# Two attention layers on one Trainium2 core: regrouping transfers per pair of heads, issued with the copy, and a shorter lag

## The chip, the cores and the metric

The kernel runs on one core of one Trainium2 chip (trn2). All data is float32. The metric is the device time of one execution in microseconds (us). The time before is 4608.19 us, the median of three runs (4605.17 to 4620.24).

## The reference

The input x is (8, 512, 32, 32): 8 images of 512 channels and 1024 positions. Two layers follow each other. Each normalizes its input by groups of 16 channels and adds its output to what came in. Layer 0 is ordinary attention with 8 heads of 64 channels. Layer 1, which the change is about, mixes the heads of the scores before the softmax and normalizes each head's attention matrix after it. Cut to what matters:

```python
def _L1_conv_ref(x, w_q, w_k, w_v, w_head, in_gamma, in_beta, w_proj, b_proj):
    q = jnp.einsum('oc,bct->bot', w_q, xf).reshape(b, heads, hd, t)   # k, v alike
    attn = jnp.einsum('bhdq,bhdT->bhqT', q, k) * scale
    attn = jnp.einsum('gh,bhqT->bgqT', w_head, attn)
    attn = jax.nn.softmax(attn, axis=-1)
    # mean and variance over both axes of each head, then gamma and beta
    attn = (attn - mean) / jnp.sqrt(var + EPS)
    attn = attn * in_gamma[None, :, None, None] + in_beta[None, :, None, None]
    out = jnp.einsum('bhqT,bhdT->bhqd', attn, v).reshape(b, t, c)
    out = out @ w_proj.T + b_proj

x = x + _L0_conv_ref(_gn(x), ...)
x = x + _L1_conv_ref(_gn(x), ...)
```

The mixing of heads, `bhqT->bgqT`, is what shapes the kernel: for each pair of a query and a key the 8 scores of the 8 heads are multiplied by an 8 x 8 matrix.

## The kernel before

The order of the work on each engine is the order in which the program writes it down; no scheduler moves it. Layer 0 runs for all images first, then layer 1 for all images, with the projections of the next image laid between the end of one image and the beginning of the next.

**Layer 1 of one image.** The work is cut into tiles of queries and keys: QB = 256 queries (4 blocks, qb) by KB = 256 keys (4 blocks, kb), so 16 tiles t per image. Each t takes two half steps x = 2t and 2t + 1; there are NX = 32 of them. In a half step PE computes scores of four heads: scores(x, 0) and scores(x, 1) take one pair of heads hp each. One call fills one PSUM tile of 128 x 1024 with 128 partitions of queries, two heads, two groups j of 128 queries, and 256 keys. The queries are laid out so that partition p of the scores is c * 64 + i * 8 + r, with c of 2, i of 8 and r of 8.

**Raw.** The scores leave PSUM for SBUF as they are, into `raw` (line 1204): one tile [128, 8 heads, 2, 256] for a whole t, of which there are two. The copy (lines 1207 and 1209) is on ACT, or on DVE for scores(x, 0) of the first MLAG half steps and of odd ones.

**Regrouping.** To mix heads with a matmul the 8 heads have to lie on partitions. `regroup(t)` (line 1211) does this with 8 SBUF-to-SBUF transfers from the queue of SyncE (SP), one for each r: it reads 16 partitions of `raw` (those with this r, a stride of 8), 16 KB each, and writes 128 partitions (c, i, head) of a tile `re`, 2 KB each. Each r has a tile of its own; there are 16 of them, for two t. All 8 are issued together in the odd half step, after scores(x, 1). The order of r is R_ORDER = (0, 4, 1, 5, ...).

**Mix.** `mix(y, j)` (line 1220) multiplies a piece of `re` by the constant `wmix`, which holds w_head for 8 queries on the diagonal, in 32 small matmuls of 64 x 64 (64 in the profile, since a float32 matmul appears as two) into another PSUM tile. ACT then takes the exponential (line 1237). Mix and exponential belong to half step y = x - MLAG with MLAG = 4, so they run four half steps after the scores of the same data.

**Sums and values.** One half step later still, w = x - MLAG - 1, ACT squares the exponentials (line 1247), DVE adds up the exponentials and their squares (lines 1254 and 1258), and PE multiplies the exponentials by v (`values`, line 1276) into two accumulators. After 8 half steps a block of queries is finished: `totals` sums over the keys with PE, the totals go through a small tile `row` to a column layout by transfers, `reciprocals` and `divide` follow 2 and 5 half steps later, and `leave` takes the accumulators out in the first half step of the next block (four copies on ACT, four on DVE).

**Buffers.** All PSUM tiles of layer 1 but the accumulators come from one pool of three (`m_psum`): scores, mix, totals and projections take turns in the order in which they are written down, so each waits until the reader of the third tile before it is done. The transfers of SP run in the order of the program, and the queue stops at a transfer whose data is not ready.

**Ends of images.** After the last scores there are MLAG + 1 half steps without scores. In the last of the slots 32 to 35 the projection of k for the next image is put (`k_half`, two per slot); `k_leave` copies it out in the next half step.

Of the kernel before, what the change touches and what calls it, by code (L numbers as in the profile page):

```python
# [9 lines left out]
F32 = mybir.dt.float32  # L10
# [8 lines left out]
P = 128  # L19
# [448 lines left out]
def tile_two_attention_layers(  # L468
# [19 lines left out]
    nc = tc.nc  # L488
    B, C, T = x_d.shape
    H = w_head.shape[0]  # L490
    D = C // H
# [6 lines left out]
    NR = 8  # L498
# [17 lines left out]
    def const_tile(name, shape, dt=F32):  # L516
        return const.tile(shape, dt, tag=name, name=name)
# [11 lines left out]
    ident = const_tile("ident", [P, P])  # L529
# [18 lines left out]
    nc.vector.tensor_add(mask8, m2[:, 0], m2[:, 1])  # L548
    nc.vector.tensor_scalar_mul(mask8, mask8, S1)
    eye8 = const.tile([H, P // H, H], F32, tag="eye8", name="eye8")  # L550
    nc.vector.tensor_copy(eye8, ident[:H, :H].unsqueeze(1).to_broadcast([H, P // H, H]))
    whr = const_tile("whr", [P, H])
    with tc.tile_pool(name="ps_w", bufs=1, space=PSUM) as ps_w:
        pw = ps_w.tile([P, H], F32, tag="w", name="pw")
# [49 lines left out]
    class GroupStats:  # L604
# [3 lines left out]
        def __init__(self, pool, psum, mv, nm, keep=3):  # L608
            self.keep = keep
            self.pool, self.psum, self.mv, self.nm = pool, psum, mv, nm  # L610
            self.w = mv.shape[1]
# [384 lines left out]
    with ExitStack() as l1:  # L996
        ypool = l1.enter_context(tc.tile_pool(name="ypool", bufs=1))
        qopool = l1.enter_context(tc.tile_pool(name="qopool", bufs=1))
        kvpool = l1.enter_context(tc.tile_pool(name="kvpool", bufs=1))
        rawpool = l1.enter_context(tc.tile_pool(name="rawpool", bufs=2))  # L1000
        wtpool = l1.enter_context(tc.tile_pool(name="wtpool", bufs=1))
        repool = l1.enter_context(tc.tile_pool(name="repool", bufs=2 * NR))
        epool = l1.enter_context(tc.tile_pool(name="epool1", bufs=2))
        e2pool = l1.enter_context(tc.tile_pool(name="e2pool", bufs=3))
        zpool = l1.enter_context(tc.tile_pool(name="zpool1", bufs=1))
# [6 lines left out]
        KB = 2 * P  # L1012
        NKB = T // KB
        NX = 2 * NQB * NKB
        QLAG = NX // NQB
        R_ORDER = (0, 4, 1, 5, 2, 6, 3, 7)
        MLAG = 4

        def m_psum(nm):
            return ps_m.tile([P, 2, FB], F32, tag="m", name=nm)  # L1020
# [15 lines left out]
        def load_y(b, chunks=range(NCC)):  # L1036
            for c in chunks:
                if c == 0:
                    y_t[b] = ypool.tile([P, NCC, T], F32, tag="y", name=f"y_{b}")
                nc.sync.dma_start(out=y_t[b][:, c], in_=x1_d[b][ts(c, P), :])  # L1040
# [47 lines left out]
        def k_leave():  # L1088

            for b, oc, ps in k_half.due:  # L1090
                nc.scalar.copy(k_t[b][:, oc, :FB], ps[:, 0])
                nc.vector.tensor_copy(k_t[b][:, oc, FB:], ps[:, 1])
            k_half.due = []
# [88 lines left out]
        class Attention1:  # L1182
            def __init__(self, b):
                self.b = b
                self.raw, self.re, self.e, self.e2 = {}, {}, {}, {}

            def scores(self, x, i):

                b, t, hp = self.b, x // 2, x % 2 * 2 + i
                qb, kb = t // NKB, t % NKB  # L1190
                nm = f"s1_{b}_{x}_{i}"
                ps = m_psum(nm)
                pv = ps.rearrange("p m (j k) -> p m j k", j=2)
                for j in range(2):
                    for c in range(2):
                        for m in range(2):
                            r = slice(m * D, m * D + D)
                            nc.tensor.matmul(  # L1198
                                pv[c * D : c * D + D, m, j],
                                qo_t[b][r, 2 * qb + j, hp, ts(c, D)],  # L1200
                                k_t[b][r, hp, ts(kb, KB)], start=True, stop=True,
                            )
                if x % 2 == 0 and i == 0:
                    self.raw[t] = rawpool.tile([P, H, 2, KB], F32, tag="raw", name=f"raw_{b}_{t}")
                dst = self.raw[t][:, 2 * hp : 2 * hp + 2]
                if i == 0 and (x < MLAG or x % 2):
                    nc.vector.tensor_copy(dst, pv)  # L1207
                else:
                    nc.scalar.copy(dst, pv)  # L1209

            def regroup(self, t):

                raw = self.raw.pop(t)
                for r in R_ORDER:
                    self.re[t, r] = repool.tile(
                        [P, 2, KB], F32, tag="re", name=f"re_{self.b}_{t}_{r}"
                    )
                    nc.sync.dma_start(out=self.re[t, r], in_=raw[r::NR])

            def mix(self, y, j):  # L1220

                t, kc = y // 2, y % 2
                if j == 0:
                    self.e[y] = epool.tile([P, 2, T], F32, tag="e", name=f"e1_{self.b}_{y}")
                ps = m_psum(f"m1_{self.b}_{y}_{j}")
                for r in R_ORDER:
                    for c in range(2):
                        k0 = kc * P + c * D
                        for a in range(2):
                            rows = slice(a * D, a * D + D)  # L1230
                            nc.tensor.matmul(  # L1231
                                ps[c * D : c * D + D, a, ts(r, D)],
                                self.re[t, r][rows, j, k0 : k0 + D],
                                wmix[rows].rearrange("p g i -> p (g i)"),
                                start=True, stop=True,
                            )
                nc.scalar.activation(self.e[y][:, j], ps.rearrange("p a c -> p (a c)"), AF.Exp)  # L1237
# [151 lines left out]
            def half_step(self, x, ag):  # L1389
                y, w = x - MLAG, x - MLAG - 1  # L1390
                first = 0 < w < NX and w % QLAG == 0
                if first:

                    self.scores(x, 0)
                    self.leave(w // QLAG - 1)
                if 0 <= w < NX:
                    self.squares(w, 0)
                    self.sum_e(w, 0)
                if x < NX and not first:
                    self.scores(x, 0)  # L1400
                if 0 <= w < NX:
                    self.squares(w, 1)
                    self.sum_e(w, 1)
                k_leave()
                if 0 <= w < NX:
                    self.sum_e2(w, 0)
                    self.sum_e2(w, 1)
                if 0 <= y < NX:
                    self.mix(y, 0)
                if x < NX:  # L1410
                    self.scores(x, 1)
                    if x % 2:
                        self.regroup(x // 2)
                if 0 <= y < NX:
                    self.mix(y, 1)
                if 0 <= w < NX:
                    self.values(w)
                    self.e.pop(w)
                    if w % QLAG == QLAG - 1:
                        qb = w // QLAG  # L1420
                        self.totals(qb)
                        if qb < NQB - 1:
                            ag.at(x + 2, lambda: self.reciprocals(qb))
                            ag.at(x + 5, lambda: self.divide(qb))
                ag.run(x)
# [18 lines left out]
        for b in range(B):  # L1444
            more = b + 1 < B
            a = Attention1(b)
            ag = Agenda()
            for i in range(NV):
                ag.at(1, lambda i=i: v_pair(b, NV + i))
            if more:  # L1450
                for c in range(NCC):
                    ag.at(6 + 2 * c, lambda c=c: load_y(b + 1, [c]))
                    ag.at(14 + 2 * c, lambda c=c: load_w(("k", b + 1), wkT, [c]))
                    ag.at(22 + 2 * c, lambda c=c: load_w(("v", b + 1), wvT, [c]))
                    ag.at(24 + c, lambda c=c: normalize1(b + 1, [c]))
                for i in range(2 * NCC):
                    ag.at(NX + i // 2, lambda i=i: k_half(b + 1, i))
            for x in range(NX + MLAG + 1):
                a.half_step(x, ag)

            a.leave(NQB - 1)
            a.reciprocals(NQB - 1)
            a.instance()
            ag.flush()
            if more:
                v_pair(b + 1, 0)
            a.instance_end()
            a.divide(NQB - 1)
            for g in range(H):
                a.affine(g)  # L1470
            if more:
                load_w(("q", b + 1), wqT)
                v_pair(b + 1, 1)
            for oc in range(NCC):
                out1(b, oc)
            if more:
                for oc in range(NCC):
                    q_chunk(b + 1, oc)
# [69 lines left out]
```

## Time and profile before

| | |
|---|---|
| median of three runs | 4608.19 us |
| profiled execution, span | 4622.4 us |
| mean granted TensorE clock | 0.988 |
| layer 1 begins at about | 1985 us |
| PE busy, 200 to 1850 us (layer 0) | 1637.43 of 1650 us |
| PE busy, 1985 to 4622 us (layer 1) | 2411.75 of 2637 us |
| DMA engines busy, layer 0 and layer 1 | 9% and 53% |

In the profile L1231 is line 1231 of the kernel. A row such as "m L1231" is the instruction that writes the PSUM tile m (mix); s is scores, a the accumulators, t the totals, e the exponentials. PE is the matmul, PEld its weight load, SPq an issue by SP. "idle before, releaser" is time in which the engine stood still just before such an instruction, and what ended it; "issue" means that the engine waited for nothing that the profile shows. The costliest rows of the mixing stage are:

```profile
L1231 PE MATMUL m<-wmix,re 64*64 64x64 f32 x32768 | 615.0, 220 | 156.4 <-issue 133.0
L1237 ACT ACTIVATE e<-m 128x1024 f32<-128x1024 f32 x512 | 528.4, 1037 | 180.5 <-PE m L1231 179.6
L1198 PE MATMUL s<-k,q 64*64 64x256 f32 x8192 | 555.8, 386 | 12.6 <-issue 5.6
L1276 PE MATMUL a<-e,v 128*64 128x256 f32 x4096 | 532.0, 400 | 28.3 <-issue 28.3
L1209 ACT COPY raw<-s 128x1024 f32<-128x1024 f32 x368 | 374.3, 1019 | 135.7 <-PE s L1198 102.0
re<-raw SPq DMA_DIRECT2D x1024, 256.0 KB
```

### The profile page before, as it was taken

The numbers are of one execution on the slowest core, as the hardware profiler recorded it, in microseconds if no ns is written. First come the engines' busy times: TensorE is split into PE (matmuls) and PEld (weight loads), VectorE is DVE, ScalarE is ACT, GpSimd is POOL, SyncE is SP. The second block draws the span as 40 slices with busy tenths as digits, with TensorE's granted clock in tenths as the row PEclk, the third lists the DMA queues.
The fourth block names the chain that finished last, engine by engine and source line by source line (L and its number), as shares of the span: only waits on it lengthen the run. The fifth ranks groups of instructions, "written<-read, shape, count | busy, mean of one in ns | idle before, by whom it ended". The sixth has DMA issues, their size and how long they took to land.

```text
span 4622.4 us, 129851 instructions
## 1 busy us (share of the span) xinstructions
PE 4346.5 (94%) x58552; PEld 2261.2 (49%) x58552; DVE 2465.1 (53%) x3384; ACT 2258.8 (49%) x2623; POOL 6.6 (0%) x14
## 2 busy tenths in 40 slices
PE   7999999999999999889989989989989998989987
PEld 3343434343434343456466466465465465565564
DVE  1727272727272727257367367376266376376375
ACT  1717171717171716067267177276276275275374
POOL 0000000000000000000000000000000000000000
PEclk9999999999999999999999999999999999999999
DMA  2010101010101000267176275275375374474373
GB/s 73 17 40 16 41 18 39 18 39 18 39 18 39 18 21 18 75 167 180 54 191 154 69 182 147 86 183 130 95 173 130 106 181 111 118 181 122 102 176 103
DMA packets 242307, 426.37 MB, mean 92 GB/s; under 512 B 63056, under 2 KB 63056, under 8 KB 241744
## 3 DMA queue, kind: packets, MB, share of 16 engines
q1 hardware_dynamic: 239168, 413.77, 33.7%
q8 instruction: 460, 7.54, 0.7%
q10 hardware_dynamic: 2304, 4.20, 0.3%
q14 instruction: 103, 0.84, 0.1%
q0 software_dynamic: 272, 0.02, 0.0%
HBM read 114.32 MB, written 34.08 MB: 32 GB/s over the span
## 4 chain that ended last, share of the span: by engine, by line
PE 86%; issue 5%; ACT 4%; DMA 2%; DVE 2%; SPq 1%; ACTq 0%; POOL 0%; DVEq 0%; POOLq 0%
PE a L1276 9%; PE a L876 9%; PE m L1231 9%; PE s L850 9%; PE s L1198 8%; PE pk L1081 5%; PE pk L797 5%; PE pp L1167 5%; PE pv L1105 5%; PE pq L1137 5%; PE pq L797 5%; PE pv L820 5%; PE pp L797 5%; PE t L1306 2%; PE z L898 1%
## 5 line engine op out<-in xcount | busy, mean ns | idle before, releaser
L1231 PE MATMUL m<-wmix,re 64*64 64x64 f32 x32768 | 615.0, 220 | 156.4 <-issue 133.0
L1231 PEld LDWEIGHTS m<-wmix,re 64*64 64x64 f32 x32768 | 592.2, 135 | 260.2 <-issue 171.2
L1237 ACT ACTIVATE e<-m 128x1024 f32<-128x1024 f32 x512 | 528.4, 1037 | 180.5 <-PE m L1231 179.6
L1258 DVE TENSOR_TENSOR z<-z,e 128x1024 f32<-128x1024 f32 x448 | 534.3, 1219 | 93.3 <-ACT e L1247 93.1
L855 ACT ACTIVATE e<-s 128x1024 f32<-128x1024 f32 x512 | 498.4, 1026 | 148.5 <-PE s L850 148.5
L1254 DVE TENSOR_TENSOR z<-z,e 128x1024 f32<-128x1024 f32 x448 | 537.6, 1218 | 57.4 <-ACT e L1237 57.2
L1198 PE MATMUL s<-k,q 64*64 64x256 f32 x8192 | 555.8, 386 | 12.6 <-issue 5.6
L1276 PE MATMUL a<-e,v 128*64 128x256 f32 x4096 | 532.0, 400 | 28.3 <-issue 28.3
L850 PE MATMUL s<-q,k 64*64 64x512 f32 x4096 | 489.8, 592 | 3.0 <-ACT e L855 1.5
L863 DVE TENSOR_TENSOR zacc<-zacc,e 128x1024 f32<-128x1024 f32 x384 | 469.5, 1223 | 41.8 <-ACT e L855 15.3
L876 PE MATMUL a<-e,v 64*64 64x512 f32 x4096 | 484.2, 589 | 0.0
L1247 ACT ACTIVATE e<-e 128x1024 f32<-128x1024 f32 x448 | 464.5, 1071 | 0.0
L1209 ACT COPY raw<-s 128x1024 f32<-128x1024 f32 x368 | 374.3, 1019 | 135.7 <-PE s L1198 102.0
L1198 PEld LDWEIGHTS s<-k,q 64*64 64x64 f32 x8192 | 282.9, 135 | 195.7 <-issue 90.5
L1276 PEld LDWEIGHTS a<-e,v 128*64 128x64 f32 x4096 | 284.0, 141 | 177.1 <-issue 57.3
L876 PEld LDWEIGHTS a<-e,v 64*64 64x64 f32 x4096 | 156.8, 133 | 282.6 <-issue 282.6
L850 PEld LDWEIGHTS s<-q,k 64*64 64x64 f32 x4096 | 152.3, 133 | 286.6 <-issue 261.1
L1207 DVE COPY raw<-s 128x1024 f32<-128x1024 f32 x144 | 176.2, 1224 | 174.7 <-PE s L1198 171.7
L1081 PE MATMUL pk<-y,wk 128*128 128x512 f32 x512 | 230.7, 605 | 5.6 <-DVE y L1066 5.0
L1167 PE MATMUL pp<-q,wp 128*128 128x512 f32 x512 | 223.7, 598 | 7.2 <-ACT q L1385 7.2
L797 PE MATMUL pk<-n,w 128*128 128x512 f32 x512 | 226.0, 600 | 4.2 <-issue 4.2
L797 PE MATMUL pp<-xa,wp 128*128 128x512 f32 x512 | 224.2, 599 | 5.9 <-DVE xa L938 5.9
(174 smaller groups left out, 3266.5 us busy)
## 6 DMA issues: line engine op xcount, KB each, us to landing
re<-raw SPq DMA_DIRECT2D x1024, 256.0 KB
x<-in_x_dram SPq DMA_DIRECT2D x32, 512.0 KB
rzb<-zd SPq DMA_DIRECT2D x128, 128.0 KB
x<-x SPq DMA_DIRECT2D x32, 512.0 KB
y<-x SPq DMA_DIRECT2D x32, 512.0 KB
rzb<-zd SPq DMA_DIRECT2D x64, 256.0 KB
xs<-x SPq DMA_DIRECT2D x32, 512.0 KB
out_dram<-xs SPq DMA_DIRECT2D x32, 512.0 KB
```

Source lines behind the costliest of these rows:

```text
L797: nc.tensor.matmul(ps[:, f], w[:, c, o0 + oc * P : o0 + (oc + 1) * P], rhs[:, c, ts(f, FB)], start=(c == 0), stop=(c == NCC - 1),)
L850: nc.tensor.matmul(ps[c * D : c * D + D, m], k[r, hp, k0 : k0 + D], q[r, hp, ts(f, FB)], start=True, stop=True,)
L855: nc.scalar.activation(e[i], ps, AF.Exp)
L863: nc.vector.tensor_add(zacc[g], zacc[g], e[i])
L876: nc.tensor.matmul(acc[g][a][m * D : m * D + D], v[rows, kc, ts(2 * hp + m, D)], e[i][rows, m], start=(kc == 0), stop=(kc == NG - 1),)
L1198: nc.tensor.matmul(pv[c * D : c * D + D, m, j], qo_t[b][r, 2 * qb + j, hp, ts(c, D)], k_t[b][r, hp, ts(kb, KB)], start=True, stop=True,)
L1231: nc.tensor.matmul(ps[c * D : c * D + D, a, ts(r, D)], self.re[t, r][rows, j, k0 : k0 + D], wmix[rows].rearrange("p g i -> p (g i)"), star ...
L1237: nc.scalar.activation(self.e[y][:, j], ps.rearrange("p a c -> p (a c)"), AF.Exp)
L1247: nc.scalar.activation(e2, self.e[y][:, j], AF.Square)
L1254: nc.vector.tensor_add(self.z[:, j], self.z[:, j], self.e[y][:, j])
L1258: nc.vector.tensor_add(self.z2[:, j], self.z2[:, j], self.e2[j])
L1276: nc.tensor.matmul(self.acc[w][two * D : two * D + D, s].rearrange("p (c i) -> p c i", i=Q8), v_t[b][:, kc, ts(g, D)], e[:, g], start=(kc ...
```

## The change

The regrouping is turned round and cut up by heads. Each call of scores now has a `raw` tile of its own, [128, 2 heads, 2, 256], of which there are four, and issues two transfers right after its copy: for each of its two heads, 128 partitions of `raw` (2 KB each) go to 16 partitions of `re` (16 KB each). `re` is one tile per t, [128, 8 r, 2, 256], of which there are three. A transfer thus starts as soon as two heads are copied and no longer when all eight are. Since the two heads of a pair are four partitions apart in the new layout, the constant from which `wmix` is made is permuted to match. With the data regrouped sooner, the lag of the mix is set to three half steps. Then the last `k_half` falls into the last half step, and a `k_leave()` after it takes its result out.

```diff
     eye8 = const.tile([H, P // H, H], F32, tag="eye8", name="eye8")
-    nc.vector.tensor_copy(eye8, ident[:H, :H].unsqueeze(1).to_broadcast([H, P // H, H]))
+    nc.vector.tensor_copy(
+        eye8.rearrange("q i (two hp) -> q i two hp", two=2),
+        ident[:H, :H].rearrange("q (hp two) -> q two hp", two=2).unsqueeze(1).to_broadcast(
+            [H, P // H, 2, H // 2]
+        ),
+    )
...
-        rawpool = l1.enter_context(tc.tile_pool(name="rawpool", bufs=2))
+        rawpool = l1.enter_context(tc.tile_pool(name="rawpool", bufs=4))
...
-        repool = l1.enter_context(tc.tile_pool(name="repool", bufs=2 * NR))
+        repool = l1.enter_context(tc.tile_pool(name="repool", bufs=3))
...
-        R_ORDER = (0, 4, 1, 5, 2, 6, 3, 7)
-        MLAG = 4
+        MLAG = 3
...
-                if x % 2 == 0 and i == 0:
-                    self.raw[t] = rawpool.tile([P, H, 2, KB], F32, tag="raw", name=f"raw_{b}_{t}")
-                dst = self.raw[t][:, 2 * hp : 2 * hp + 2]
+                raw = rawpool.tile([P, 2, 2, KB], F32, tag="raw", name=f"raw_{b}_{x}_{i}")
                 if i == 0 and (x < MLAG or x % 2):
-                    nc.vector.tensor_copy(dst, pv)
+                    nc.vector.tensor_copy(raw, pv)
                 else:
-                    nc.scalar.copy(dst, pv)
+                    nc.scalar.copy(raw, pv)
 
-            def regroup(self, t):
-
-                raw = self.raw.pop(t)
-                for r in R_ORDER:
-                    self.re[t, r] = repool.tile(
-                        [P, 2, KB], F32, tag="re", name=f"re_{self.b}_{t}_{r}"
-                    )
-                    nc.sync.dma_start(out=self.re[t, r], in_=raw[r::NR])
+                if x % 2 == 0 and i == 0:
+                    self.re[t] = repool.tile([P, NR, 2, KB], F32, tag="re", name=f"re_{b}_{t}")
+                for two in range(2):
+                    nc.sync.dma_start(out=self.re[t][two * 4 + hp :: H], in_=raw[:, two])
...
-                for r in R_ORDER:
+                for r in range(NR):
...
-                                self.re[t, r][rows, j, k0 : k0 + D],
+                                self.re[t][rows, r, j, k0 : k0 + D],
...
-                    if x % 2:
-                        self.regroup(x // 2)
...
             a.leave(NQB - 1)
+            k_leave()
             a.reciprocals(NQB - 1)
```

More of the change, by code (lines that the diff above doesn't have):

```diff
@@ L1184, in __init__ @@
                 self.b = b
-                self.raw, self.re, self.e, self.e2 = {}, {}, {}, {}
+                self.re, self.e, self.e2 = {}, {}, {}
             def scores(self, x, i):
@@ L1202, in scores @@
                             )
-                if x % 2 == 0 and i == 0:
-                    self.raw[t] = rawpool.tile([P, H, 2, KB], F32, tag="raw", name=f"raw_{b}_{t}")
-                dst = self.raw[t][:, 2 * hp : 2 * hp + 2]
-                if i == 0 and (x < MLAG or x % 2):
-                    nc.vector.tensor_copy(dst, pv)
-                else:
-                    nc.scalar.copy(dst, pv)
-            def regroup(self, t):
-                raw = self.raw.pop(t)
-                for r in R_ORDER:
-                    self.re[t, r] = repool.tile(
-                        [P, 2, KB], F32, tag="re", name=f"re_{self.b}_{t}_{r}"
-                    )
-                    nc.sync.dma_start(out=self.re[t, r], in_=raw[r::NR])
+                raw = rawpool.tile([P, 2, 2, KB], F32, tag="raw", name=f"raw_{b}_{x}_{i}")
+                if i == 0 and (x < MLAG or x % 2):
+                    nc.vector.tensor_copy(raw, pv)
+                else:
+                    nc.scalar.copy(raw, pv)
+                if x % 2 == 0 and i == 0:
+                    self.re[t] = repool.tile([P, NR, 2, KB], F32, tag="re", name=f"re_{b}_{t}")
+                for two in range(2):
+                    nc.sync.dma_start(out=self.re[t][two * 4 + hp :: H], in_=raw[:, two])
             def mix(self, y, j):
```

## The prediction

> **What bounds the kernel now.** I read, in this order: busy shares, the chain of waits, the waits of layer 1, then the timeline of a few half steps beside the DMA rate.
>
> ```profile
> PE 4346.5 (94%) x58552; PEld 2261.2 (49%) x58552; DVE 2465.1 (53%) x3384; ACT 2258.8 (49%) x2623; POOL 6.6 (0%) x14
> PE 86%; issue 5%; ACT 4%; DMA 2%; DVE 2%; SPq 1%; ACTq 0%; POOL 0%; DVEq 0%; POOLq 0%
> q1 hardware_dynamic: 239168, 413.77, 33.7%
> q8 instruction: 460, 7.54, 0.7%
> ```
>
> PE is the bound, so only PE's idle time can be won. Summed from the trace, it is idle 268 us, 218 of them from 1985 us on, in layer 1. The second largest share of the chain, "issue", is time in which PE waits for no semaphore. The waits of layer 1 (2010 to 4550 us) say the same (engine, line, who was waited for, us, times, longest):
>
> ```profile
> PE m L1231 <- issue: 128.4, 94, 4.6
> PE a L1276 <- issue: 27.3, 19, 2.6
> PE m L1231 <- ACT raw L1209: 17.8, 26, 0.7
> PE t L1306 <- DVE z L1258: 5.2, 7, 0.7
> PE s L1198 <- ACT e L1237: 5.2, 20, 0.3
> PE m L1231 <- DMA re<-raw: 3.0, 5, 0.7
> ```
>
> Waiting for regrouped data costs 3 us; the nameless "issue" costs over 160. The timeline shows one such gap, here in the middle of a run of 16 matmuls:
>
> ```profile
> 2700.30 6.76 SPq L1218 DMA_DIRECT2D re<-raw  x8
> ...
> 2705.63 0.43 PE L1276 MATMUL a<-e,v 128*64 128x256 f32 x1
> ...
> 2707.34 1.94 PE L1276 MATMUL a<-e,v 128*64 128x256 f32 x15 [1.27 <-issue]
> ```
>
> In the trace's packet records a 16 KB packet of q8 ran from 2704.91 to 2705.87, and PE went on 1.47 us after its end. The same holds for 124 of the 125 long gaps: PE resumes 1.3 to 1.5 us after a q8 packet ends. 460 packets of 256 instructions are PE's 117,104 records: these are its instruction fetches, one in three arrives too late, and they cost 163 us.
>
> Then I asked what makes a fetch late. Counting PE's records, every 256th marks the point from which a fetch can be asked for; the lag from there to its packet's start is 0.94 us (median) in layer 0, where the DMA engines are 9% busy, and 3.23 us (mean) in layer 1. In layer 1 it is 1.2 us (median) where no data moved in the 2 us before, and 3.9 us where over 230 GB/s moved. Mean stall per fetch by lag: 0.01 us at 1 to 1.5 us, 0.05 at 1.5 to 2, 0.19, 0.37, 0.40, 0.89 in the next half microseconds, 0.55 at 4 to 5, 0.98 above 5. So a fetch queues behind regrouping data. The DMA view of the same 14 us, 2700 to 2714, shows the form of the load (40 slices, busy tenths):
>
> ```profile
> DMA  0000699999999899999999999999998982111001
> ```
>
> Eight transfers (2 MB) at 250 GB/s fill the engines for 8.3 us, a 512 KB load follows, then they rest.
>
> [...] 2 KB packets of regrouping take 0.133 us, those of the weights from HBM, which go to 128 partitions, 0.084.
>
> **The change, part by part.**
> (a) Transfers turned round. Before, a transfer read 16 partitions and wrote 128; now it reads 128 and writes 16. Number (1024), bytes (256 KB) and 2 KB runs are the same, and so is the stride of 8 on the narrow side[...]. No row shows a write to 16 partitions. From both sides: 0.084 us a packet[...] and, if writes suffer more than reads, 0.18 us (the 95th percentile of before). I take 0.133, unchanged.
> (b) Issue in pairs after each copy instead of eights after two half steps. A half step takes 6.8 us now (190 us between first mix and last score for 28 of them), so 512 KB come every 3.4 us and need 2.1 us. The backlog then falls to nothing before the next pair: the lag should lie between 1.2 (idle) and 1.2 + 2.1 plus what a load adds, about 1.2 to 3.8, where it reached 5 to 9 for 59 fetches. Equal weight on the six half-microsecond bins from 1 to 4 gives (0.01 + 0.05 + 0.19 + 0.37 + 0.40 + 0.89)/6 = 0.32 us; times 362 fetches, 115 us. Saved: 163 - 115 = 48 us. Ends: 0, if the lag does not shorten, and 110, if it stays under 2.5 us.
> (c) Waits for transfers. The copies waited 27.4 us on ACT for eights to leave raw; hidden except for 3 us on PE. Four small buffers give each copy two half steps; three regrouped tiles free the transfer from waiting for the mix of the same half step. -3 us. Before, the first mix of a tile had its eight waits spread over its matmuls; now all stand ahead of the first. That is some 3 more waiting instructions of 51 ns per tile, 128 tiles, 20 us at most, but the sequencer meets them 0.6 us ahead of the engine: 0. Behind a waiting mix stand only PE's own matmuls; the last pair has some 9 us (rest of a half step, a whole one, and one scores) for 1.1 us of issue, 1 us to the first packet and 2.1 us of data, so no wait.
> (d) Lag 3. The oldest tile is used one half step earlier, and work with period 8 moves from odd to even half steps. Once in 8, ACT also empties accumulators (4 copies, 1.50 us). On an odd step DVE copies raw and ACT starts these at once; on an even step ACT's raw copy (1.01 us) stands in front. Walking one such step from its start with the timeline's durations: row copy to 1.45, raw copy to 2.46, accumulators to 3.96, two squares to 6.0, exp to 7.0. PE would have finished values at 5.8, and its next scores need the buffer of that exp: it waits 1.2 us, with 0.4 for the accumulators and 0.7 at a later raw copy, 2.3 us. Before, the same places cost 0.28 + 0.74 = 1.02. So 1.3 us x 24 = 31 us more at worst; where a late fetch falls into the same steps it hides them. I take 12, ends 0 and 31.
> (e) One half step fewer in the fill, k_leave() at the end, the permuted wmix: PE is 100% busy at image ends, with k projections behind the drain; the last image swaps one drain step (5.1 us, DVE-bound) and one of scores (1.9) for a full one (6.8). 0.
>
> Sum: -48 - 3 + 12 = -39; 4608 - 39 = 4569, say 4570 us.
>
> **The rivals.**
> A. The load stays as dense: 1 MB per half step plus loads keeps the engines as busy as now, and the lag as long. For it: a burst's first 1.5 us run at 152 to 184 GB/s, so pairs may never reach 250. Then only (c) and (d) remain: -3 + 12 to 31, so 4617 to 4636; 4622.
> B. Writing to 16 partitions is slower: at 0.18 us a packet, 1 MB takes 5.8 us of 6.8, loads make it full, mix waits for data. 128 tiles x some 0.5 us = +64: 4672, say 4670. Against it: both sides show the same stride.
> C. Fetches become nearly free: -110 - 3 + 12: 4507. ACT does not forbid it: 5.75 us per half step (2 exp, 2 squares, 1.5 copies) plus 0.2 is still under 6.4.
>
> **How the numbers follow.** Forecast 0.52, A 0.22, B 0.12, C 0.14. Time: the forecast's, 4570. Range: down to 4505 takes in C, up to 4640 takes in A; B and the tails are left out. Within 0.3% is 4594 to 4622. Faster: 0.47 of the forecast's 0.52 and C: 0.61. Same: 0.05 of the forecast and half of A: 0.16. Slower: the rest of A and B: 0.23.
>
> **What would show it.** Right: "PE m <- issue" and "PE a <- issue" together fall from 156 to about 110 us while q8 stays at 460 packets; the DMA slices show short rests every 3 us; "s <- ACT e" grows from 5 to 15 us or more. Wrong: these two rows stay (A), "PE m <- DMA re<-raw" grows to tens of us or packets get longer (B), or PE waits for "ACT raw" in every half step, which I cost at nothing.

## The result, and the profile after

The changed kernel takes 4681.49 us (median of four runs, 4678.73 to 4689.24) against 4606.68 for the kernel before: a ratio of 1.0159, with a 95% interval from 1.0135 to 1.0183. It is slower by 75 us, where 4570 was forecast, and it lies outside of the range given.

Busy shares, the chain by engine and two DMA queues of the changed kernel, from its page (span 4687.4 us, 65 more than before):

```profile
PE 4368.7 (93%) x58552; PEld 2277.1 (49%) x58552; DVE 2460.6 (52%) x3384; ACT 2262.6 (48%) x2623; POOL 6.6 (0%) x14
PE 86%; issue 5%; ACT 4%; DMA 2%; DVE 1%; SPq 0%; POOL 0%; DVEq 0%; ACTq 0%; POOLq 0%
q1 hardware_dynamic: 239168, 413.77, 33.3%
q8 instruction: 462, 7.57, 0.7%
```

The same work and the same bytes; nothing new has taken a large share. So the loss lies in two terms: PE is busy for 22 us longer with the same 58,552 matmuls, and idle for 43 us more (span less busy). The waits of PE in layer 1, 2010 to 4550 us (who waited, for whom, us, times, longest):

```profile
PE m L1229 <- issue: 139.7, 91, 5.7
PE a L1274 <- issue: 35.2, 24, 3.9
PE s L1202 <- ACT e L1235: 25.7, 23, 1.1
PE s L1202 <- issue: 8.9, 13, 2.1
PE m L1229 <- ACT raw L1211: 5.9, 12, 0.7
PE t L1304 <- DVE z L1256: 5.2, 7, 0.7
PE m L1229 <- DMA re<-raw: 4.3, 5, 1.3
```

The two "issue" rows, which were to fall from 156 to 110 us, stand at 175. The wait of scores for the exponential has grown from 5.2 to 25.7, that of mixes for ACT's raw copy has fallen from 17.8 to 5.9, and waiting for regrouped data costs no more than before.

For all comparisons below, layer 1 is taken from its first scores to the end of the profiled execution and split into nameless gaps of PE over 150 ns (the late fetches), its waits for a named releaser, and the rest, in which PE works. "Half" is the time in that stretch in which the record of the granted clock reads 0.5. All in us, summed from the traces:

```
                     layer 1   fetches   waits     rest     half
before                2658.6     167.5    49.6   2441.5     96.0
after                 2724.0     198.7    62.0   2463.3    146.8
a_eights              2706.2     206.5    57.3   2442.4    116.0
a_lag4_ring           2662.7     156.0    74.2   2432.5     95.8
a_lag4_eights         2701.3     209.3    41.7   2450.3    129.1
b_lag3                2767.4      23.5   224.3   2519.6    205.0
b_no_transfers        2429.8      12.6    50.4   2366.8     34.1
b_pad32               2641.2     167.8    45.1   2428.3     65.0
b_pad64               2645.7     152.6    50.1   2443.0     92.4
a_pad64               2723.2     203.3    61.4   2458.5    139.9
a_lag4_ring_pad64     2667.0     151.2    79.1   2436.7     94.5
```

From before to after: fetches +31, waits +12, rest +22, together the 65 us of the span. The 22 us are the half clock: if PE's working time in layer 1 that falls into stretches at half clock is counted half, 2396 us are left before and 2394 after (an estimate from the traces and their clock record). Two programs whose fetches fall at the same instructions (before and b_pad64, after and a_pad64; see "Is it placement?") differ by up to 15 us in the fetches and 13 in the layer, so smaller differences between two rows tell nothing.

How a late fetch costs twice is seen in the changed kernel just after the last scores of an image. First the timeline of PE (start, us, instruction, idle before), then the same stretch cut along the steps of the clock record (us, busy of PE, PEld, DVE, ACT, POOL, clock, DMA share, GB/s):

```profile
2532.44 1.16 PE L1229 MATMUL m<-wmix,re 64*64 64x64 f32 x64
2533.39 1.07 PE L1202 MATMUL s<-k,q 64*64 64x256 f32 x16
2534.26 0.86 PE L1229 MATMUL m<-wmix,re 64*64 64x64 f32 x42
2537.50 0.57 PE L1229 MATMUL m<-wmix,re 64*64 64x64 f32 x22 [2.38 <-issue]
2538.00 2.72 PE L1274 MATMUL a<-e,v 128*64 128x256 f32 x16
2540.65 2.41 PE L1229 MATMUL m<-wmix,re 64*64 64x64 f32 x90
2545.08 0.81 PE L1229 MATMUL m<-wmix,re 64*64 64x64 f32 x38 [2.02 <-issue]
2545.82 3.63 PE L1274 MATMUL a<-e,v 128*64 128x256 f32 x16
```

```profile
2535.62:2539.03 3.41, 1.53 (x32) 1.18 (x34) 2.83 (x3) 0.90 (x1) 0.00 (x0) 1.00 1.05 220
2539.03:2542.44 3.41, 3.41 (x78) 2.31 (x78) 3.25 (x3) 2.01 (x3) 0.00 (x0) 0.50 1.08 231
2542.44:2545.86 3.42, 1.40 (x74) 1.19 (x67) 2.52 (x3) 1.02 (x1) 0.00 (x0) 1.00 0.67 150
2545.86:2549.27 3.41, 3.41 (x19) 1.71 (x16) 1.23 (x1) 2.92 (x3) 0.00 (x0) 0.50 0.02 5
```

The scores have ended at 2534.5, but the DMA engines are still full with regrouping (220 and 231 GB/s in the first two windows), and a fetch whose packet ends at 2536.08 lets PE stand for 2.38 us in the middle of a mix. That leaves the window 2535.62 to 2539.03 with only 1.53 us of work, and in the next window TensorE is granted half its clock. The same happens again in the second pair of windows: there 16 matmuls of values take 3.63 us, where they take 1.95 us at full clock.

### The profile page after: what moved, and what is told of

Its sections match the earlier page's. It is cut to its first block, busy times and chain, and to the rows that moved or that the text cites. A ratio compares the mean times of both kernels' runs of the same rounds, so it can differ in the third digit from the quotient of the medians.

```text
span 4687.4 us, 129322 instructions
## 1 busy us (share of the span) xinstructions
PE 4368.7 (93%) x58552; PEld 2277.1 (49%) x58552; DVE 2460.6 (52%) x3384; ACT 2262.6 (48%) x2623; POOL 6.6 (0%) x14
## 4 chain that ended last, share of the span: by engine, by line
PE 86%; issue 5%; ACT 4%; DMA 2%; DVE 1%; SPq 0%; POOL 0%; DVEq 0%; ACTq 0%; POOLq 0%
PE m L1229 9%; PE a L1274 9%; PE a L881 9%; PE s L855 9%; PE s L1202 9%; PE pk L1085 5%; PE pk L802 5%; PE pp L1171 5%; PE pv L1109 5%; PE pq L1141 5%; PE pq L802 5%; PE pv L825 5%; PE pp L802 5%; DMA re<-raw 2%; PE t L1304 1%
## 5 line engine op out<-in xcount | busy, mean ns | idle before, releaser
L1274 PE MATMUL a<-e,v 128*64 128x256 f32 x4096 | 549.7, 408 | 37.9 <-issue 36.1
```

The lines of the kernel that those rows point to most:

```text
L1274: nc.tensor.matmul(self.acc[w][two * D : two * D + D, s].rearrange("p (c i) -> p c i", i=Q8), v_t[b][:, kc, ts(g, D)], e[:, g], start=(kc ...
```

## The experiments

Times are medians; ratios are against runs of the kernel before on the same chip. L stands for "the lag of 3 is the loss", T for "the turned transfers are the loss".

**Lag 4 again, first try.** The changed kernel with

```diff
-        MLAG = 3
+        MLAG = 4
```

> The changed kernel with a lag of 4 instead of 3; the new transfers stay. Theory L (the lag is the loss: period-8 work on even steps, and the first steps without scores meet transfers still in flight): 45 us or more of the 75 lost come back, about 4615 to 4635; "s <- ACT e" falls from 27 to under 8 us and the nameless PE gaps from 195 to about 165. Theory T (the new transfers are the loss, they keep the DMA engines from resting and instruction fetches late): 4660 or more, nameless gaps stay above 185.

4707.92 us, 1.0216 (1.0193 to 1.0240): slower still. But this run does not say what it was made for. Its waits of PE (2010 to 4550 us) have a row that is as long in no other kernel:

```profile
PE m L1229 <- ACT e L1235: 95.5, 100, 3.1
PE m L1229 <- issue: 90.5, 73, 4.6
```

In the built program the three PSUM buffers are no longer taken in turn: 112 of the 512 mixes (not half of the tiles, as an expectation below has it) get the buffer of the tile two before, whose exponential is not done. In the kernels before and after each buffer comes back after exactly three tiles. The lag was measured together with that.

**VectorE's copy on even steps, first try.** In the changed kernel

```diff
-                if i == 0 and (x < MLAG or x % 2):
+                if i == 0 and (x < MLAG or x % 2 == 0):
```

> The changed kernel with the DVE copy of scores(x, 0) on even half steps instead of odd ones, so that in the step that empties the accumulators ACT has no raw copy in front. Theory L's first half (ACT overloaded in the same step): "s <- ACT e" falls from 27 to under 10 us and the time by 10 to 25 us, to 4657 to 4672. If that wait was only in the place of late fetches: the row falls, the time stays within 5 us of 4681.

4679.14 us, 1.0167 (1.0150 to 1.0184). The scores' wait for the exponential fell to 12.0, but mixes now wait 23.1 for it and 17.6 for ACT's copy. Here 48 PSUM tiles came back after two; the same fault.

**Eights in place of pairs.** The changed kernel, all transfers of a tile written down together after the odd step, in the same direction, with eight copy buffers and two regrouped tiles (cut to what matters):

```diff
-                for two in range(2):
-                    nc.sync.dma_start(out=self.re[t][two * 4 + hp :: H], in_=raw[:, two])
+                if x % 2 and i:
+                    for h4, rw in enumerate(self.raws):
+                        for two in range(2):
+                            nc.sync.dma_start(out=self.re[t][two * 4 + h4 :: H], in_=rw[:, two])
```

> The changed kernel (lag 3, new direction) with all eight transfers of a tile issued together after the odd half step, as before the change. If pairs are what delays fetches, the nameless gaps fall from 195 towards 165 and the time to about 4640. If direction and lag matter and pairs do not: 4670 to 4700, or slower still where the mix then waits for the last transfer ("m <- DMA re" above 20 us).

4675.34 us, 1.0162 (1.0131 to 1.0194), fetch gaps 207 us. The edit does not do what it was made for. SP goes through its own list, and in this direction each transfer waits for the copy of its own pair alone. So the eight do not come as a block: the median tile has 5.5 of its 8 transfers issued before its last copy is done, with pairs it is 6, and the last issue follows the last copy by 1.7 us, with pairs by 1.6. In the kernel before none is issued before the last copy, and the last follows it by 7.0 us. The run shows that it hardly matters where these lines stand in the program; of the grain of the issue, on which the forecast rested, it says little.

**No transfers.** In the kernel before all mixes read the first tile, and only that one is transferred; the scores of the other tiles are left out of the result.

> The kernel before without the regrouping transfers: those of the first tile of the first image are made, every mix reads that tile, so all mixed scores but those are wrong. If the nameless PE gaps of layer 1 are instruction fetches held up behind regrouping: they fall from 164 to under 30 us and the time to 4440 to 4490. If fetches are late for another reason (matmuls too dense for the fetch itself): the gaps stay above 100 us, the time above 4550.

4394.55 us, 0.9543 (0.9527 to 0.9559). With the waits of PE:

```profile
PE m L1233 <- ACT raw L1211: 17.8, 24, 0.7
PE m L1233 <- issue: 9.9, 16, 1.3
```

The regrouping costs 211 us, though the kernel before shows only 3 us of waiting for it. Fetch gaps fall from 167.5 to 12.6, and the rest by 75 with 62 us less at half clock. That the late fetches are the transfers' doing is shown by this run. Of the 75 us some 33 are what PE works longer at half clock (counted as above, an estimate); where the other 42 come from was not found, so not all of the 211 us are late fetches.

**Lag 4 with the PSUM buffers in turn.** The changed kernel with MLAG = 4 and three tags of one buffer each (cut to what matters):

```diff
+        turn = []
+
         def m_psum(nm):
-            return ps_m.tile([P, 2, FB], F32, tag="m", name=nm)
+            turn.append(nm)
+            return ps_m.tile([P, 2, FB], F32, tag=f"m{len(turn) % 3}", name=nm)
```

> The changed kernel with a lag of 4 half steps again, and the three PSUM buffers of the scores and mixes taken strictly in turn (three tags of one buffer each), so that each is used again after three tiles, as in the kernels before and after; the run with lag 4 alone had half of them used again after two. Theory L (the lag of 3 is the loss: ACT's order on even steps, and a shorter way for the transfers to be late): 4595 to 4620, and the wait of a score for the exponential on ACT falls from 26.8 us to under 8. Theory T (the turned transfers are the loss: writes to 16 partitions at a time lengthen the packets and with them the instruction fetches): 4660 to 4690, with nameless gaps of TensorE in layer 1 still 180 to 200 us. Both half: 4630 to 4650.

4628.27 us, 1.0046 (1.0029 to 1.0063). Most of the loss is gone; L holds for some 52 of the 75 us. Waits of PE, then those of ACT, both 2010 to 4550 us:

```profile
PE m L1232 <- issue: 118.1, 80, 4.5
PE m L1232 <- ACT raw L1214: 37.2, 34, 3.3
PE s L1205 <- ACT e L1238: 6.5, 23, 0.3
```

```profile
ACT raw L1214 <- DMA re<-raw: 36.0, 21, 3.8
```

The fetches stand at 156 us, 11 under the kernel before, which is less than two programs with the same placement differ by: that pairs help at this lag is not shown. What they cost is seen in the copies, which wait for one of the four buffers to be read out, mostly in the first half steps of an image, where scores follow each other without mixes; PE then waits for the copy up to 3.3 us.

**Lag 3 alone, in the kernel before.**

```diff
-        MLAG = 4
+        MLAG = 3
...
             a.leave(NQB - 1)
+            k_leave()
```

> The kernel before with a lag of 3 half steps alone (and the call of k_leave at the end of an image that it brings); the transfers stay as they were, eight for each tile, issued after the odd step, each reading 16 partitions. Theory L: 4665 to 4690, with a wait of scores for the exponential of 20 to 30 us and nameless gaps of about 190. Theory T: 4600 to 4630, of which about +20 for that same wait, and nameless gaps still near 164. A third, that the pool of a tile is late with this lag because the eight are issued only after the odd step: a wait of the first mix for its transfers of over 20 us, and 4640 or more whatever else.

4732.77 us, 1.0280 (1.0242 to 1.0318), the slowest of the first eight. Of the three expectations the third holds:

```profile
PE m L1231 <- DMA re<-raw: 156.7, 266, 2.0
PE m L1231 <- issue: 15.6, 21, 2.0
```

From the last issue for a tile to its first mix there are 9.9 us before and 1.7 here (medians from the trace), so mixes wait for data, and while they do the fetches catch up: their gaps fall to 23.5 us. In the changed kernel, where transfers start with the copies, that interval is 8.8 us again. The new issue is what makes a lag of 3 bearable, but the lag of 3 is not worth having.

**Even steps, PSUM in turn.** The edit of the second experiment together with that of the fifth.

> The changed kernel with VectorE's copy of the first pair on the even steps rather than the odd, so that ACT has no copy of scores before the accumulator's four copies, and the three PSUM buffers strictly in turn. If the 21.5 us of added wait of scores for the exponential come from ACT's copy standing in front of the accumulator's copies, that row falls from 26.8 to under 8 us and the time to 4650 to 4665. If it only moves to another row (a mix that waits for the exponential or for ACT's copy on odd steps), the time stays at 4675 to 4685.

4677.77 us, 1.0153 (1.0113 to 1.0192). Scores wait 11.9 us for the exponential instead of 25.7, mixes 20.6 for ACT's raw copy instead of 5.9: the sum stays. The wait only moves, as the second expectation had it.

**Reciprocals' transfers on GpSimd.** In the changed kernel:

```diff
-                nc.sync.dma_start(out=zd, in_=rz)
+                nc.gpsimd.dma_start(out=zd, in_=rz)
...
-                    nc.sync.dma_start(
+                    nc.gpsimd.dma_start(
                         out=self.rzb[two * D : two * D + D], in_=zd[two].partition_broadcast(D)
```

> The changed kernel with the transfers of the reciprocals (to DRAM and back, once for each quarter of an image) issued by GpSimd in place of SyncE, so that SyncE doesn't hold the pairs of transfers while it waits for the first of them to land. If the bunched issue after such waits, above all at the end of the scores, feeds the extra fetch stalls there (38.9 us against 9.8 at 210 to 240 us of each image), these fall back to 10 to 20 us and the time to 4650 to 4665. If the stalls there come from the transfers that remain while the mixes run without scores, nothing changes: 4675 to 4685.

4656.25 us, 1.0118 (1.0078 to 1.0158): 25 less, or 19 by the ratios, whose intervals overlap. The fetch gaps in the 20 us after the last scores went from 32.8 to 19.3, inside the first expectation.

The same edit in the kernel before:

> The kernel before with the transfers of the reciprocals issued by GpSimd. In the changed kernel this took 25 us off. If it works by keeping SyncE free of the 100 us for which it waits on the first of these transfers (103.8 us here too), then the kernel before gains less, since only one group of eight in every two half steps can be held: ratio 0.996 to 0.999. If it works by anything at the end of an image, which both kernels have, it gains as much: 0.993 to 0.996. If the gain was chance: 0.999 to 1.001.

4684.04 us, 1.0190 (1.0167 to 1.0212): 88 more, which no expectation held. A part is plain: at the end of an image the last reciprocals come later, and the projection waits for the divided result ("pp" for "ACT q") 23.0 us instead of 7.2. Half-clock time rises to 156.5. Why the edit gains in one kernel and loses in the other was not settled.

**The direction alone, as it was meant.** Eights as above, a lag of 4, PSUM in turn, eight copy buffers and two regrouped tiles.

> The transfers turned round and nothing else: the changed kernel's eight transfers for each tile issued together after the odd step, with eight buffers of a pair's copy and two regrouped tiles (in bytes the buffers of the kernel before), a lag of 4 and the PSUM buffers strictly in turn. Pairs with lag 4 stood at 1.0046 of the kernel before, and there the copies waited 66.7 us for a pair's buffer to be read out (ACT 39.6, VectorE 27.1), which put some 20 us on TensorE. If that wait is the whole cost of pairs at lag 4, this run has a ratio of 0.998 to 1.002 and a wait of mixes for ACT's copy of 15 to 20 us. If writing to 16 partitions costs something of itself, the ratio is 1.003 to 1.010 with nameless gaps above 165 us.

4670.17 us, 1.0171 (1.0153 to 1.0190). The copies wait for nothing, and yet the gain does not come. The ratio lies above both expectations, the gaps above 165 us as the second had it. The run holds a second change that was overlooked. SP's largest wait for these transfers is:

```profile
SPq L1223 <- PE m L1236: 465.0, 96, 10.4
```

With two regrouped tiles, each one tile for all r, the eight must wait until the last mix of the tile two before is done (in the kernel before SP waits 140.8 us for mixes). They then come as one block: issues end from 0.5 to 6.2 us after the last copy, where pairs with lag 4 end at 1.5. But the block of the kernel before stands in much the same place, 0.6 to 7.0 us, and has 167.5 us of fetch gaps to 209 here; pairs in this direction and at this lag have 156. So turned transfers may cost something that pairs win back, or the wait for whole tiles costs it. No run separates the two, and a worth of the direction or of the grain is neither shown nor excluded. With the edit for GpSimd on top:

> Both together: transfers turned round, in eights, lag 4, the reciprocals' transfers on GpSimd. If the two parts add: the ratio of the first run of this call less 0.002 to 0.005, so 0.994 to 0.999, faster than both kernels. If not, it stays with the first.

4738.44 us, 1.0300 (1.0276 to 1.0324), slower again; the parts do not add.

**Is it placement?** Fetches fall at every 256th instruction of PE: in the changed kernel there are 462 packets of 16 KB for 117,773 records of PE's instructions, and with the records counted in blocks of 256 from the first, 136 of the 197 gaps of PE over 150 ns in layer 1 end at instruction 194 or 195 of a block (199 of 261 us; before 130 of 196, 169 of 217 us). A small matmul of the setup is repeated 64 or 32 times more, to shift all later boundaries. But a float32 matmul is four instructions of PE in the trace, two weight loads and two matmuls (32,768 of each for the 16,384 of the mixes), where the expectations count two. So 32 shift the boundaries by half a block, and 64 by a whole one, which leaves them where they were: the first scores of layer 1 are instruction 227 of their block with 64 and without.

```diff
-        nc.tensor.matmul(pw, eye8.rearrange("p i h -> p (i h)"), whT, start=True, stop=True)
+        for _ in range(1 + 64):
+            nc.tensor.matmul(
+                pw, eye8.rearrange("p i h -> p (i h)"), whT, start=True, stop=True
+            )
```

> The kernel before with one small matmul of the setup repeated 64 times more (128 instructions of TensorE, half a block of 256; a few microseconds of work at the start). If placement against the block boundaries matters little: ratio 0.999 to 1.004. If it is what most differences in this study are: outside 0.990 to 1.008, with nameless gaps that differ from 163 us by more than 20.

> The same with 32 more (a quarter of a block). Placement of little matter: 0.999 to 1.003. Otherwise another value than both the kernel before and the one with 64.

> The changed kernel with the 64 small matmuls. If the loss of 1.6% belongs to the change and not to the placement: 1.012 to 1.020. If placement rules: outside of that, as far down as 1.005.

> The changed kernel with lag 4 and PSUM buffers in turn (1.0046) with the 64 small matmuls. If pairs with lag 4 are truly better than the eights with lag 4 (1.0171): 1.002 to 1.008. If its 1.0046 was a lucky placement: 1.010 to 1.020.

Ratios: 1.0051 (1.0028 to 1.0074), 1.0035 (1.0022 to 1.0047), 1.0204 (1.0170 to 1.0237) and 1.0115 (1.0083 to 1.0147). The matmuls themselves cost more than was thought: layer 1 starts 27 us later with 64 and 13 with 32, which is 0.0058 and 0.0028 of the time. Less that, the ratios are 0.9993, 1.0007, 1.0146 and 1.0057, close to 1, 1, 1.0159 and 1.0046 without the shift. As measured, all four lie outside what was expected if placement matters little, three of them by little, the fourth among the values for a lucky placement; that the start accounts for it was seen afterwards.

The run with 32 is the only one that moves the boundaries, and in the kernel before this is worth little. The other three repeat their kernels. For the changed kernel its own trace answers: its eight images begin at eight different places of a block (instruction 227, 175, 123, 71, 19, 223, 171, 119), those of the kernel before and of lag 4 are as spread, and from the first scores of one image to those of the next it takes 338 us on average before (334 to 342), 347 after (340 to 354) and 338 with pairs and lag 4 (333 to 341). One lucky placement does not make that. The loss belongs to the change, and most of it to the lag: with the 64 matmuls too, lag 3 has 203 us of fetches and lag 4 has 151.

## Why the prediction was wrong

Its sum, term by term, against the 65 us between the two profiles:

```
step                                      forecast   measured
(b) fetches, without the ends of images        -48         +8
(c) waits for transfers                         -3         +1
(d) ACT's order at a lag of 3                  +12         +9
(e) ends of images (fetches there)               0        +23
    other named waits                            -         +2
    rest: TensorE at half clock                  -        +22
sum                                            -39        +65
```

**Step (b) failed**, in the words "The backlog then falls to nothing before the next pair". The fetch lag stayed (3.23 us before, 3.28 after), and fetches asked for with nothing outstanding were no more frequent: 111 of 366 before, 87 of 365 after (bytes count as outstanding from the start of their issue to the end of their packet). The working counted 2.1 us of data per 3.4 us at 250 GB/s, 38% rest. While the transfers of an image run, the engines rest 21% of the time before and 19% after, since they move 220 GB/s and 210 GB/s when they move, and loads come on top. The load stayed as dense as rival A had it. At a lag of 4 the pairs stand 11 us of fetches under the kernel before, not 48, and with the 64 matmuls 1 us, while the named waits, those for the four copy buffers above all, are 25 us longer. The upper end of the step, 110 us for a lag under 2.5 us, does not follow from its own bins either: they give (0.01 + 0.05 + 0.19)/3 = 0.08 us a fetch and a saving of 133 us. Nothing came of it, since the lag did not shorten.

**Step (e) failed** as well. It held the ends free because PE was 100% busy there. In the 20 us after the last scores, fetch gaps sum to 9.8 us over the eight images before and 32.8 after. All kernels with turned transfers and a lag of 3 have 19 to 33 us there, those with a lag of 4 and the transfers in place between 5 and 15. What sets the limit there is read from the timeline above and not tested by itself: mixes run without scores and use up instructions faster (64 matmuls of a mix in 1.16 us, 16 of scores in 1.07), while the last transfers still fill the engines.

**Missing was the price of a long gap.** Half-clock time grew by 51 us and PE's working time by 22; at a lag of 4 with PSUM in turn both fell back. No step had it. Together with the ends of images it is why even rival A, with 4617 to 4636, lies too low. Rival B's 4670 is nearest to the measured time, but by luck: its sign, mixes that wait for transfers for tens of us, did not appear (4.3 us).

**Step (d)** came out near by luck: the wait for the exponential grew by 20.5 us, over the 12 taken, and that for the raw copy, which the working kept, fell by 12. **Step (c)** was right in that these waits are next to nothing. **Step (a)** was taken, as an estimate, as unchanged at 0.133 us a packet; why these packets take longer than the weights' with 0.084 us was not shown. The median went from 0.132 to 0.140 us, the mean from 0.1318 to 0.1322, and the rate while any engine moves from 220 to 210 GB/s. It is 205 to 213 GB/s in the eleven kernels with the new direction and 218 to 221 in the five with the old one, 5% less: a part of rival B. What it costs by itself was not measured; with pairs, the direction and the waits of the copies together come to 0.5%.

So the change is two changes: pairs in the new direction, about +20 us, and the lag of 3, about +52 (1.0159 less 1.0046; 41 with the 64 matmuls in both). From the run with lag 4 to the changed kernel, layer 1 grows by 61 us in the profiles: fetches +43, of which 24 at the ends of images, named waits -12, and +31 in the rest with 51 us more at half clock. Why the other 19 us of fetches come with the lag stays open; so does the effect of the edit for GpSimd. No version that does the whole work beats the kernel before.

## What to carry to other kernels

A transfer on which hardly anybody waits (3 us here) may still cost much (211 us here), in good part through instruction fetches that come late while it runs (their gaps fall from 167.5 to 12.6 us without it); a run without the transfers prices it at once. Smaller issues of the same bytes did not shorten the lag of fetches here, where the engines stayed busy four fifths of the time. When a constant such as a lag is put back for an experiment, look at how the buffers rotate in both programs before a difference is given a cause. And look in the trace whether an edit did what it was made for: the eights were not issued as eights, and the 64 matmuls shifted nothing.

## What the runs showed of the hardware

The clock record has two values, 1.0 and 0.5, and moves in steps of 3.413 us (24 stretches at 0.5 before and 37 after, most of them one step long). Taking from eleven traces all windows of layer 1 that follow one at full clock, sorted by the share of the window before in which PE was idle:

```
idle in the window before   windows   then at half clock
under 0.40                     7484        0
0.40 to 0.50                    223        1
0.50 to 0.55                     70       20
0.55 to 0.60                     73       53
over 0.60                       177      177
```

The window before need not be idle throughout: between 50% and 60% of idleness 73 of 143 windows are followed by half clock, above 60% all of 177. So a gap of 2 us in one window (59% of it) is mostly enough, and the window after it then costs up to 1.7 us of matmul time (an estimate, half of 3.413).

Fetch lag grows with what is outstanding on the queue of the transfers. In the changed kernel it is 1.7 us with nothing outstanding, 2.8 to 3.4 with up to 0.8 MB, 5.3 with 0.8 to 1.0 MB and 6.9 with more (means, counted as above). A fetch with a lag under 2 us costs less than 0.1 us there, one with a lag over 5 us 1.5 us.
